# Gated graph network and graph attention, 64 graphs: layer 1's values by seven block products in place of eight, a later norm and half words for the younger pair, and shared small buffers

## The chip, the cores and the metric

The kernel runs on one core of one Trainium2 chip. The metric is the device time of one execution in microseconds (us). A NeuronCore has a matrix engine (TensorE, PE in the profile; its weight loads are listed apart as PEld), a vector engine (VectorE, DVE), a scalar engine (ScalarE, ACT), a third elementwise engine (GpSimd, POOL) and a queue that issues DMAs (SyncE, SP). Each takes its own instructions in program order and waits on semaphores for the others. Below, "the chip's time" is the median of three runs, and "span" is what the hardware profiler saw of one execution.

## What is computed

There are 64 graphs of 256 nodes with 256 features each, in float32, and an integer adjacency matrix for each. Two layers follow each other, both with a layer norm and a relu ahead and a residual behind. Layer 0 is a gated graph network of three steps (messages, an aggregation over the edges, a GRU cell); layer 1 is graph attention with four heads of 64 features.

```python
h = jnp.maximum(_layernorm(x), 0.0)
x = x + L0(h, adj, ...)             # 3 x: m = h @ weight[i]; aggr = A^T m; h = gru(aggr, h)
h = jnp.maximum(_layernorm(x), 0.0)
h = (h @ W.T + b).reshape(B, 256, 4, 64)                    # layer 1's values
logits = leaky_relu(l_src[:, :, None] + l_dst[:, None], 0.2)   # l_src, l_dst: h with a_src, a_dst
probs = softmax(where(adj == 1, logits, -9e15), axis=2)
x = x + einsum('bijh,bjhc->bihc', probs, h)
```

The change concerns the line of layer 1's values. The kernel computes it with the scores in one product: the weights `w_val` have VW = 268 columns, four times 64 value columns and a column that gives the softmax denominator, and eight more for `l_src` and `l_dst`.

## The kernel before

Graphs go in pairs (PB = 2 graphs, 512 nodes, KN = 2 blocks of 128 nodes in each graph, KD = 2 blocks of 128 features); there are 32 pairs. Nothing is scheduled by a tool: each piece of work is a Python function that is put down with a tick, a phase and a pair (`at`, L340), and at the end all pieces are emitted tick by tick; within a tick first STEP, then READY, then REST, and within a phase the younger pair first. The order in which an engine meets its instructions is thus written out by hand. Pairs follow each other by 18 ticks (`APART`). A pair needs three steps of six ticks in layer 0 (`Step.tick_0` to `tick_5`, at its ticks 0 to 5, 12 to 17 and 24 to 29), and the next pair's steps fill the gaps, so every tick holds one STEP.

A tick's STEP is mostly PE: blocks of four float32 products of 128x128 by 128x256 (`block`, L327) and single ones (`part`, L463). `tick_2` (L516) ends with a chain over three engines: PE writes `qb` from `hT`, DVE adds bias and a kept term to it into `hn` (L524), ACT then writes another quarter of `hn` from the same bank (`state_n`, L466). READY and REST carry the work of other pairs beside it: `back` (L882) turns a state back into rows on PE (`pback`, L900), after which ACT casts it (`hNhi`, L890) and DVE takes the rest (`hNlo`, L891).

The values of pair p (all but the last three pairs, 29 of 32: `dma_b`) are at its ticks 43 and 44, in REST, where pair p+1 is in `tick_1` and `tick_2` of its last step, and pair p+2 in its `back`:

```python
for r in (r0, r0 + 1):                                  # values, L950
    pt = bank(f"pv_{p}_{r}")
    for k in range(KD):
        nc.tensor.matmul(pt[:, :VW], hb["hT"][:, k, ts(r, P)], w_val[:, k, :], ...)   # L960
    nc.vector.scalar_tensor_tensor(v["val"][:, r, :], pt[:, :VW], rstd, b_val, ...)    # L965
nc.vector.tensor_copy(v["score"][:, r0 : r0 + 2, :], v["val"][:, r0 : r0 + 2, S0:])    # L973
```

The relu'd rows come from DMA transposes: `plan_norm` gives `xn`, `plan_turn` splits it into half words (`words`, L401), writes them to DRAM, reads them back transposed into the buffer `turned` (SP, L407) and joins them (`hT`, L413). At tick 45 `score_rows` follows: PE transposes the scores (`pscore`, L983), DVE copies them to `flat` (L985), and SP writes them to DRAM and reads them back on all partitions (`drow`, L1003). They feed the maxima (`any`, L1045) from tick 49 on.

At the same ticks 43 to 46 of pair p stands the layer 0 norm of pair p+3, three pairs younger: at its own tick -10 the normed rows (L367), at -9.5 their relu on ACT (L859), at -9 the half words (L401), at -8 the transposing read and at -3 the join.

Small buffers: `any` (the maxima's unused full output) and `flat` have one buffer each; `o` (a quotient that DVE writes, L611, and POOL adds to x, L616) has two; the tags of the `small` pool have four.

Of the kernel before, what the change touches and what calls it, by code (L numbers as in the profile page):

```python
# [9 lines left out]
F32 = mybir.dt.float32  # L10
# [8 lines left out]
P = 128  # L19
# [8 lines left out]
def gated_gnn_then_gat_kernel(  # L28
# [47 lines left out]
    PB = 2  # L76
# [2 lines left out]
    VC = C + 1  # L79
    S0 = H * VC  # L80
    VW = S0 + 2 * H
    NPAIR = B // PB

    assert PB == 2 and KD * N == 512
# [178 lines left out]
    a_exp = const.tile([P, KD, 2 * H], F32, name="a_exp")  # L263

    bcol = const.tile([P, KD], F32, name="bcol")
    nc.gpsimd.memset(a_exp, 0.0)
    nc.gpsimd.memset(b_val, 1.0)

# [22 lines left out]
    def value_weights():  # L291
        pts = [bank(f"pwv_{k}") for k in range(KD)]
        pa = bank("pwa")
        for k in range(KD):
            for g in range(KD):
                nc.tensor.transpose(pts[k][:, ts(g, P)], w_nat[:, g, ts(k, P)], ident)
        for k in range(KD):
            for g in range(KD):
                nc.tensor.matmul(
                    pa[:, ts(k, 2 * H)], w_nat[:, g, ts(k, P)], a_exp[:, g, :],  # L300
                    start=(k == 0 and g == 0), stop=(g == KD - 1), skip_group_check=True,
                )
        for k in range(KD):
            nc.tensor.matmul(
                pa[:, ts(KD, 2 * H)], bmat[0][:, k, :], a_exp[:, k, :],
                start=False, stop=(k == KD - 1), skip_group_check=True,
            )
        for k in range(KD):
            nc.vector.tensor_copy(
                w_val[:, k, :S0].rearrange("q (h c) -> q h c", h=H)[:, :, :C],  # L310
                pts[k][:, :D].rearrange("q (h c) -> q h c", h=H),
            )
            nc.vector.tensor_copy(w_val[:, k, S0:], pa[:, ts(k, 2 * H)])
        nc.vector.tensor_copy(b_val[:, S0:], pa[:, ts(KD, 2 * H)])


    def flat(y):
# [26 lines left out]
    def plan_norm(src, name, p, ticks, relu=False):  # L344


        v = {}

        def stats(r0):
            def fn():  # L350
                if not v:
                    v["st"] = small.tile([P, R, 6], F32, tag="st", name=f"st_{name}")
                    v["mv"] = small.tile([P, R, 2], F32, tag="mv", name=f"mv_{name}")
# [247 lines left out]
    def divided(p, r, v, add, scalar=False):  # L601

        heads = v["po", r][:, :S0].rearrange("q (h c) -> q h c", h=H)
        rden = small.tile([P, H], F32, tag="rden", name=f"rden_{p}_{r}")
# [16 lines left out]
    def plan_tail(t0, p, v, g, turn_back, residual):  # L621
# [13 lines left out]
                nc.scalar.activation(v["link"][:, i, :, :], pt, AF.Identity, scale=1 / 16)  # L635

        def stats(i):
            st = small.tile([P, KN, 6], F32, tag="st", name=f"st_b{p}_{i}")
            mv[i] = small.tile([P, KN, 2], F32, tag="mv", name=f"mv_b{p}_{i}")
# [102 lines left out]
        def maxima(i):  # L742
            for h_ in range(H):
                for r in range(i * KN, (i + 1) * KN):
                    any_ = buf("any", [P, N], f"any_{p}_{r}_{h_}")
                    nc.vector.tensor_tensor_reduce(
                        any_, two(drow[i][h_ // 2])[:, h_ % 2, :], v["noedge"][:, r, :], 1.0, -3.0e38,
                        ALU.add, ALU.max, accum_out=v["top"][:, r, h_ : h_ + 1],
                    )
            t = v["top"][:, xs[i], :]  # L750
            nc.vector.tensor_add(t, t, v["val"][:, xs[i], S0 : S0 + H])
            nc.vector.scalar_tensor_tensor(t, t, ALPHA, t, op0=ALU.mult, op1=ALU.max)
            nc.vector.tensor_scalar(t, t, barred, -1.0, op0=ALU.max, op1=ALU.mult)
# [14 lines left out]
        def last_rows():  # L768

            r, i, s, n = R - 1, PB - 1, KN - 1, H // 2  # L770
            for y in range(2):
# [8 lines left out]
                rden = small.tile([P, n], F32, tag="rden", name=f"rden_{p}_{r}_{y}")  # L780
# [47 lines left out]
    def plan_pair(p):  # L828
# [5 lines left out]
        def ready(t, fn):  # L834
            at(t0 + t, READY, p, fn)
# [16 lines left out]


        dma_a = p >= 1
        norm_ticks = (-14, -13, -13, -9.6 if p == 1 else -10) if dma_a else (-14, -13, -13, -7)
        xn_a = plan_norm(lambda: v["x"], f"a{p}", p, [t0 + t for t in norm_ticks])
        ready(-1 if p else -2.8, to_edge)
        if dma_a:
            ready(-9.5, lambda: nc.scalar.activation(flat(xn_a["xn"]), flat(xn_a["xn"]), AF.Relu))  # L859

            h = plan_turn(
                lambda: xn_a["xn"], "hT_a", f"a{p}", p, [t0 - 8.9 if p == 1 else t0 - 9, t0 - 8, t0 - 2 if p == 3 else t0 - 3],
                joins=nc.scalar.copy if p == 3 else nc.vector.tensor_copy,
            )
        else:
            h = plan_relu_T(xn_a, "hT_a", f"a{p}", p, [t0 - 4, t0 - 3])
# [86 lines left out]
        def values(r0):  # L953
            def fn():
                if r0 == 0:
                    v["val"] = buf("val", [P, R, VW], f"val_{p}")
                for r in (r0, r0 + 1):
                    pt = bank(f"pv_{p}_{r}")
                    for k in range(KD):
                        nc.tensor.matmul(  # L960
                            pt[:, :VW], hb["hT"][:, k, ts(r, P)], w_val[:, k, :],
                            start=(k == 0), stop=(k == KD - 1),
                        )
                    if dma_b:
                        nc.vector.scalar_tensor_tensor(  # L965
                            v["val"][:, r, :], pt[:, :VW], xn_b["rstd"][:, r : r + 1], b_val,
                            op0=ALU.mult, op1=ALU.add,
                        )
                    else:
                        nc.vector.tensor_add(v["val"][:, r, :], pt[:, :VW], b_val)  # L970
                if r0 == 0:
                    v["score"] = small.tile([P, R, 2 * H], F32, tag="score", name=f"score_{p}", bufs=2)
                nc.vector.tensor_copy(v["score"][:, r0 : r0 + 2, :], v["val"][:, r0 : r0 + 2, S0:])  # L973
            return fn

        rest(37 + later, values(0))
        rest(38 + later, values(2))

        def as_rows(src, n, what):

            m = R * n
            pt = bank(f"p{what}_{p}")
            nc.tensor.transpose(pt[:m, :P], flat(src), ident)  # L983
            fl = buf("flat", [m, P], f"{what}_{p}")
            nc.vector.tensor_copy(fl, pt[:m, :P])  # L985
            rows = dram.tile([PB, n, N], F32, tag=what, name=f"{what}_dram_{p}")
            for r in range(R):
# [51 lines left out]
        def maxima(r, h0):  # L1039
            def fn():  # L1040
                if r == 0 and h0 == 0:
                    v["top"] = small.tile([P, R, H], F32, tag="top", name=f"top_{p}", bufs=2)
                for h in (h0, h0 + 1):
                    any_ = buf("any", [P, N], f"any_{p}_{r}_{h}")
# [131 lines left out]
```

## Time and profile before

| | before |
|---|---|
| chip's time, median of 3 (lowest to highest) | 2470.12 us (2470.04 to 2470.18) |
| profiled execution, its own time | 2470.13 us |
| its span | 2468.3 us |
| PEld busy | 2181.3 us (88%) |
| DVE busy | 1982.7 us (80%) |
| ACT busy | 1443.9 us (58%) |
| POOL busy | 494.9 us (20%) |
| DMA | 314.77 MB, mean 128 GB/s |
| values' products, L960, pv<-w_val,hT_b | 496 records, 122.4 us |
| values' bias and scale on DVE, L965 | 116, 51.7 us |

A float32 product shows as two records on PE, since the weights are loaded twice, so the 496 records of L960 are 248 products: eight in each of 31 pairs, the last pair's being at another line. Of the execution's 2470.13 us the span covers 2468.3, and 1.8 us lie around it. [...] the distance between starts is what a product costs.

### The profile page before, as it was taken

The page shows a single profiled execution, that of the slowest core. Times are in us where ns is not written, and L with a number is a line of the kernel's source. Part 1 is how long each engine was busy: PE and PEld are TensorE (multiplying, and loading weights), DVE is VectorE, ACT ScalarE, POOL GpSimd, SP SyncE. Part 2 cuts the span into 40 slices and gives each one's busy share as a digit, 9 for nine tenths or more (in the row PEclk, how much of TensorE's full clock was granted, in tenths as well). Part 3 has the DMA queues.
Part 4 walks back from the last instruction along what each step waited for, and adds up shares of the span by engine and source line. Part 5 has one row for each costly group of instructions (what it writes and reads, how often), then busy time and mean ns, then how long its engine had stood idle before and what let it go on. Part 6 is the DMA issues. An engine that isn't in the chain of part 4 may idle for free.

```text
span 2468.3 us, 37534 instructions
## 1 busy us (share of the span) xinstructions
PE 2452.6 (99%) x13417; PEld 2181.3 (88%) x13418; DVE 1982.7 (80%) x4662; ACT 1443.9 (58%) x3025; POOL 494.9 (20%) x422
## 2 busy tenths in 40 slices
PE   9999999999999999999999999999999999999999
PEld 7888888888898888888888988888888889888888
DVE  6778887788877888877888777888778887788777
ACT  4456555655556655556555566555565555665566
POOL 0011212122121212121221212121211212121122
PEclk9999999999999999999999999999999999999999
DMA  3135565645655655656456566557564565655456
GB/s 97 43 81 130 128 155 115 154 120 124 143 132 134 143 115 129 155 118 153 117 126 144 127 139 140 117 129 150 122 153 118 125 146 123 143 134 123 98 119 135
DMA packets 324859, 314.77 MB, mean 128 GB/s; under 512 B 168688, under 2 KB 284992, under 8 KB 324672
## 3 DMA queue, kind: packets, MB, share of 16 engines
q0 software_dynamic: 33728, 130.03, 28.0%
q1 hardware_dynamic: 288576, 181.55, 27.7%
q8 instruction: 106, 1.74, 0.3%
q10 hardware_dynamic: 2368, 0.79, 0.2%
q14 instruction: 81, 0.66, 0.1%
HBM read 215.62 MB, written 57.12 MB: 110 GB/s over the span
## 4 chain that ended last, share of the span: by engine, by line
PE 83%; DVE 12%; ACT 3%; issue 1%; DMA 1%; POOL 0%; SPq 0%; ACTq 0%; DVEq 0%; POOLq 0%
PE pd L327 18%; PE pn L327 13%; PE pc L327 9%; PE po L596 9%; PE pe L327 7%; PE pa L492 5%; PE qb L463 5%; PE p L327 5%; PE pv L960 5%; PE qa L463 4%; PE pback L900 2%; DVE hT_a L582 2%; DVE R L581 2%; DVE any L1045 2%; DVE hNlo L891 1%; ACT zz L1065 1%
## 5 line engine op out<-in xcount | busy, mean ns | idle before, releaser
L327 PE MATMUL pn<-aggr,w_a 128*128 128x256 f32 x1536 | 364.9, 380 | 0.2 <-DVE pn L548 0.2
L327 PE MATMUL pd<-T,w_a 128*128 128x256 f32 x1536 | 364.5, 380 | 0.0
L563 POOL TENSOR_TENSOR R<-hT_a,hn 128x512 f32<-128x512 f32 x95 | 139.9, 1473 | 1090.5 <-ACT hn L559 1053.1
L327 PEld LDWEIGHTS pn<-aggr,w_a 128*128 128x128 f32 x1536 | 286.8, 190 | 41.3 <-issue 0.7
L327 PEld LDWEIGHTS pd<-T,w_a 128*128 128x128 f32 x1536 | 287.0, 190 | 37.0
L596 PEld LDWEIGHTS po<-val,zz 128*128 128x128 f32 x2032 | 243.2, 192 | 5.6 <-ACT zz L1080 1.1
L581 DVE SCALAR_TENSOR_TENSOR R<-Z,R 128x512 f32<-128x512 f32 x192 | 132.5, 690 | 141.8 <-POOL R L563 127.6
L616 POOL TENSOR_TENSOR x<-x,o 128x256 f32<-128x256 f32 x126 | 137.9, 1096 | 534.4 <-DVE o L611 532.1
L559 ACT ACTIVATE hn<-pn,bi 128x256 f32<-128x256 f32 x384 | 160.4, 470 | 142.9 <-PE pn L327 142.8
L596 PE MATMUL po<-val,zz 128*128 128x65 f32 x2032 | 240.5, 272 | 0.7 <-ACT zz L1080 0.7
L1065 ACT ACTIVATE zz<-zz,val 128x256 f32<-128x256 f32 x496 | 223.9, 505 | 0.5 <-DMA zz<-score_dram 0.5
L1045 DVE CUSTOM_DVE_ANT_0 any<-drow,noedge 128x256 f32<-128x256 f32 x496 | 208.2, 420 | 11.1 <-DMA drow<-score_dram 2.4
L470 ACT ACTIVATE R<-pc,brz 128x256 f32<-128x256 f32 x192 | 80.5, 470 | 220.5 <-PE pc L327 220.5
L548 DVE SCALAR_TENSOR_TENSOR pn<-R,hn 128x512 f32<-128x512 f32 x192 | 148.1, 771 | 74.7 <-ACT R L470 53.1
L470 ACT ACTIVATE R<-pe,brz 128x256 f32<-128x256 f32 x192 | 80.4, 470 | 214.0 <-PE pe L327 214.0
L327 PE MATMUL pd<-T,w_h 128*128 128x256 f32 x768 | 184.4, 383 | 3.5 <-DVE pe L532 0.5
L327 PE MATMUL p<-T,w_a 128*128 128x256 f32 x768 | 181.6, 379 | 0.0
L327 PE MATMUL pe<-aggr,w_a 128*128 128x256 f32 x768 | 181.4, 379 | 0.0
L327 PE MATMUL pc<-aggr,w_a 128*128 128x256 f32 x768 | 181.4, 379 | 0.0
L327 PE MATMUL pc<-hT_a,w_h 128*128 128x256 f32 x768 | 181.4, 379 | 0.0
L891 DVE TENSOR_TENSOR hNlo<-pback,hNhi 128x512 fp32r<-128x512 f32 x128 | 88.2, 690 | 114.1 <-ACT hNhi L890 114.1
L327 PEld LDWEIGHTS pd<-T,w_h 128*128 128x128 f32 x768 | 143.5, 190 | 33.3 <-DVE pe L532 15.0
(199 smaller groups left out, 5312.0 us busy)
## 6 DMA issues: line engine op xcount, KB each, us to landing
zz<-score_dram POOLq DMA_DIRECT2D x62, 1024.0 KB, 10.7
zz<-topT_dram POOLq DMA_DIRECT2D x62, 1024.0 KB, 8.0
adj<-in_adj_dram SPq DMA_DIRECT2D x64, 512.0 KB
drow<-score_dram SPq DMA_DIRECT2D x62, 512.0 KB
x<-in_x_dram SPq DMA_DIRECT2D x32, 512.0 KB
words_dram_a<-words_a SPq DMA_DIRECT2D x31, 512.0 KB
out_dram<-x SPq DMA_DIRECT2D x31, 512.0 KB
words_dram_b<-words_b SPq DMA_DIRECT2D x29, 512.0 KB
```

The costliest lines, as they stand in the source:

```text
L327: nc.tensor.matmul(pt[:, ts(c, N)], w[:, k, j * D + c * P : j * D + (c + 1) * P], src[:, k, :], start=start and c == 0 and k == 0, stop=(c ...
L463: nc.tensor.matmul(pt, w_n[:, j, :], src, start=start, stop=True, skip_group_check=True)
L470: nc.scalar.activation(of(dst, i)[:, c, :], src[:, c, :], AF.Tanh, bias=brz[:, g0 + c : g0 + c + 1], scale=0.5)
L492: nc.tensor.matmul(pt[:, ts(i, N)], hN[half][:, i * KN + s, ts(e, P)], edge[:, i * KN + s, :], start=(s == 0 and half == 0), stop=(s == KN ...
L548: nc.vector.scalar_tensor_tensor(by_c(self.bank(f"pn{i}")), of(self.R, i), 1.0, of(self.hn, i), op0=ALU.add, op1=ALU.mult)
L559: nc.scalar.activation(n__[:, c, :], p_n[:, c, :], AF.Tanh, bias=bi[:, 2 * KD + c : 2 * KD + c + 1])
L563: nc.gpsimd.tensor_sub(of(self.R, i), of(self.hT(), i), n__)
L581: nc.vector.scalar_tensor_tensor(d_, of(self.Z, i), 1.0, d_, op0=ALU.add, op1=ALU.mult)
L596: nc.tensor.matmul(po[:, ts(h_, VC)], zz[:, j, h_, ts(s, P)], v["val"][:, i * KN + j, ts(h_, VC)], start=(j == 0), stop=(j == KN - 1),)
L616: add(v["x"][:, r, :], v["x"][:, r, :], o)
L1045: nc.vector.tensor_tensor_reduce(any_, drow[r // KN][:, h, :], v["noedge"][:, r, :], 1.0, -3.0e38, ALU.add, ALU.max, accum_out=v["top"][:, ...
L1065: nc.scalar.activation(zz[:, h, :], zz[:, h, :], AF.Prelu, alpha=ALPHA, bias=v["val"][:, r, S0 + H + h : S0 + H + h + 1],)
```

## The change

Layer 1's values of the 29 pairs are computed by a scheme of seven products of half width. Let a graph's operand have the blocks x00, x01, x10, x11 (first index: half of the nodes, second: half of the features) and the weights w00, w01, w10, w11 (half of the features, half of the 268 columns, VH = 134). The eight block products of before (as four of 268 columns in a graph) become seven of 134 columns. Four sums of weight blocks are made once (`w_val_sum`), four sums of operand blocks in every pair (`value_sums`, for both graphs together), and the seven products land in three parts of one bank. Between them ACT copies parts from one place to another (L1007 to L1009, L1015) and DVE adds (L1016, L1024); in before the sums were made by PE's accumulation alone. The scale and bias (L1026) follow, in one operation for each of the four row blocks as before. The `score` copy is one for both graphs, at the end. The pieces stand at tick 43 (READY `value_sums`, REST `values_1` for both graphs) and 44 (READY `values_2`, REST `values_3`), and the sums use the `turned` buffer.

For pairs 3 and up the layer 0 norm's result moves from tick -10 to -8.4, its relu from -9.5 to -8.3, the half words from -9 to -7.6 and the transposing read from -8 to -6.8; the join stays. `any` and `flat` now share the two buffers of `o`; `rden`, `st`, `mv` have two buffers in place of four, `score` one in place of two.

```diff
+    VH = VW // 2
...
+        w00, w01, w10, w11 = (w_val[:, k, ts(c, VH)] for k in range(KD) for c in range(2))
+        t1, t2, t3, t4n = (w_val_sum[:, j, :] for j in range(4))
+        nc.vector.tensor_sub(t1, w01, w00)
+        nc.vector.tensor_sub(t2, w11, t1)
+        nc.vector.tensor_sub(t3, w11, w01)
+        nc.vector.tensor_sub(t4n, w10, t2)
...
-                    any_ = buf("any", [P, N], f"any_{p}_{r}_{h_}")
+                    any_ = buf("o", [P, N], f"any_{p}_{r}_{h_}")
...
+        lag = 1.6 if p >= 3 else 0
+        norm_ticks = (-14, -13, -13, -9.6 if p == 1 else -10 + lag) if dma_a else (-14, -13, -13, -7)
...
+            ready(-9.5 + 1.2 * (p >= 3), lambda: nc.scalar.activation(flat(xn_a["xn"]), flat(xn_a["xn"]), AF.Relu))
...
+                [t0 - 8.9 if p == 1 else t0 - 7.6 if lag else t0 - 9, t0 - 6.8 if lag else t0 - 8, ...],
...
+        def value_sums():
+            S = v["S"] = buf("turned", [P, 4, PB, P], f"S_{p}")
...
+            nc.vector.tensor_add(S[:, 0], x10, x11)
+            nc.vector.tensor_sub(S[:, 1], S[:, 0], x00)
+            nc.vector.tensor_sub(S[:, 2], x00, x10)
+            nc.vector.tensor_sub(S[:, 3], x01, S[:, 1])
+
+        def values_1(e):
...
+            value_product(e, 0, x[:, 0, :P], w_val[:, 0, :VH], start=True)
+            value_product(e, 2, x[:, 1, P:], w_val_sum[:, 3, :])
+            value_product(e, 1, v["S"][:, 0, e, :], w_val_sum[:, 0, :])
+            other = v["val"][:, e * KN + 1, :]
+            nc.scalar.copy(other[:, VH:], pv[e][:, ts(1, VH)])
+            nc.scalar.copy(pv[e][:, ts(1, VH)], pv[e][:, ts(0, VH)])
+            nc.scalar.copy(other[:, :VH], pv[e][:, ts(2, VH)])
+
+        def values_2(e):
+            x = hb["hT"][:, :, ts(e, N)]
+            value_product(e, 1, v["S"][:, 1, e, :], w_val_sum[:, 1, :])
+            value_product(e, 0, x[:, 1, :P], w_val[:, 1, :VH])
+            nc.scalar.copy(pv[e][:, ts(2, VH)], pv[e][:, ts(1, VH)])
+            nc.vector.tensor_add(pv[e][:, ts(1, VH)], pv[e][:, ts(1, VH)], v["val"][:, e * KN + 1, VH:])
+
+        def values_3(e):
+            value_product(e, 2, v["S"][:, 2, e, :], w_val_sum[:, 2, :])
+            value_product(e, 1, v["S"][:, 3, e, :], w_val[:, 1, VH:])
...
+            nc.vector.tensor_add(halves, halves, pv[e][:, None, 2 * VH : 3 * VH].to_broadcast([P, 2, VH]))
+            for y, src, m in ((other, other, 1), (one, pv[e][:, :VW], 0)):
+                nc.vector.scalar_tensor_tensor(
+                    y, src, xn_b["rstd"][:, r + m : r + m + 1], b_val, op0=ALU.mult, op1=ALU.add
+                )
+            if e == PB - 1:
+                v["score"] = small.tile([P, R, 2 * H], F32, tag="score", name=f"score_{p}", bufs=1)
+                nc.vector.tensor_copy(v["score"], v["val"][:, :, S0:])
+
+        if dma_b:
+            ready(43, value_sums)
+            for e in range(PB):
+                rest(43, lambda e=e: values_1(e))
+                ready(44, lambda e=e: values_2(e))
+                rest(44, lambda e=e: values_3(e))
...
-            fl = buf("flat", [m, P], f"{what}_{p}")
+            fl = buf("o", [P, N], f"{what}_{p}")[:m, :P]
```

More of the change, by code (lines that the diff above doesn't have):

```diff
@@ L265, in gated_gnn_then_gat_kernel @@
     bcol = const.tile([P, KD], F32, name="bcol")
+    w_val_sum = const.tile([P, 4, VH], F32, name="w_val_sum")
     nc.gpsimd.memset(a_exp, 0.0)
@@ L351, in fn @@
                 if not v:
-                    v["st"] = small.tile([P, R, 6], F32, tag="st", name=f"st_{name}")
-                    v["mv"] = small.tile([P, R, 2], F32, tag="mv", name=f"mv_{name}")
+                    v["st"] = small.tile([P, R, 6], F32, tag="st", name=f"st_{name}", bufs=2)
+                    v["mv"] = small.tile([P, R, 2], F32, tag="mv", name=f"mv_{name}", bufs=2)
                 for r in (r0, r0 + 1):
@@ L603, in divided @@
         heads = v["po", r][:, :S0].rearrange("q (h c) -> q h c", h=H)
-        rden = small.tile([P, H], F32, tag="rden", name=f"rden_{p}_{r}")
+        rden = small.tile([P, H], F32, tag="rden", name=f"rden_{p}_{r}", bufs=2)
         nc.vector.reciprocal(rden, heads[:, :, C])
@@ L637, in stats @@
         def stats(i):
-            st = small.tile([P, KN, 6], F32, tag="st", name=f"st_b{p}_{i}")
-            mv[i] = small.tile([P, KN, 2], F32, tag="mv", name=f"mv_b{p}_{i}")
+            st = small.tile([P, KN, 6], F32, tag="st", name=f"st_b{p}_{i}", bufs=2)
+            mv[i] = small.tile([P, KN, 2], F32, tag="mv", name=f"mv_b{p}_{i}", bufs=2)
             for s in range(KN):
@@ L779, in last_rows @@
                 heads = po[:, : n * VC].rearrange("q (h c) -> q h c", h=n)
-                rden = small.tile([P, n], F32, tag="rden", name=f"rden_{p}_{r}_{y}")
+                rden = small.tile([P, n], F32, tag="rden", name=f"rden_{p}_{r}_{y}", bufs=2)
                 nc.vector.reciprocal(rden, heads[:, :, C])
@@ L854, in plan_pair @@
         dma_a = p >= 1
-        norm_ticks = (-14, -13, -13, -9.6 if p == 1 else -10) if dma_a else (-14, -13, -13, -7)
+        lag = 1.6 if p >= 3 else 0
+        norm_ticks = (-14, -13, -13, -9.6 if p == 1 else -10 + lag) if dma_a else (-14, -13, -13, -7)
         xn_a = plan_norm(lambda: v["x"], f"a{p}", p, [t0 + t for t in norm_ticks])
@@ L858, in plan_pair @@
         if dma_a:
-            ready(-9.5, lambda: nc.scalar.activation(flat(xn_a["xn"]), flat(xn_a["xn"]), AF.Relu))
+            ready(-9.5 + 1.2 * (p >= 3), lambda: nc.scalar.activation(flat(xn_a["xn"]), flat(xn_a["xn"]), AF.Relu))
             h = plan_turn(
-                lambda: xn_a["xn"], "hT_a", f"a{p}", p, [t0 - 8.9 if p == 1 else t0 - 9, t0 - 8, t0 - 2 if p == 3 else t0 - 3],
+                lambda: xn_a["xn"], "hT_a", f"a{p}", p, [t0 - 8.9 if p == 1 else t0 - 7.6 if lag else t0 - 9, t0 - 6.8 if lag else t0 - 8, t0 - 2 if p == 3 else t0 - 3],
                 joins=nc.scalar.copy if p == 3 else nc.vector.tensor_copy,
@@ L963, in fn @@
                         )
[L964 to L970, printed above, removed]
+                    nc.vector.tensor_add(v["val"][:, r, :], pt[:, :VW], b_val)
                 if r0 == 0:
-                    v["score"] = small.tile([P, R, 2 * H], F32, tag="score", name=f"score_{p}", bufs=2)
+                    v["score"] = small.tile([P, R, 2 * H], F32, tag="score", name=f"score_{p}", bufs=1)
@@ L973, in fn @@
                 nc.vector.tensor_copy(v["score"][:, r0 : r0 + 2, :], v["val"][:, r0 : r0 + 2, S0:])
             return fn
-        rest(37 + later, values(0))
-        rest(38 + later, values(2))
+        pv = {}
+        def value_sums():
+            S = v["S"] = buf("turned", [P, 4, PB, P], f"S_{p}")
+            x00, x01, x10, x11 = (
+                hb["hT"].rearrange("q k (e m n) -> q k m e n", e=PB, m=KN)[:, k, m] for m in range(2) for k in range(KD)
+            )
[3 more added lines that the diff above has]
+            nc.vector.tensor_sub(S[:, 3], x01, S[:, 1])
@@ new lines, in value_product @@
+        def value_product(e, part, x, w, start=False):
+            nc.tensor.matmul(pv[e][:, ts(part, VH)], x, w, start=start, stop=True, skip_group_check=True)
+        def values_1(e):
+            if e == 0:
+                v["val"] = buf("val", [P, R, VW], f"val_{p}")
+            pv[e] = bank(f"pv_{p}_{e}")
+            x = hb["hT"][:, :, ts(e, N)]
[6 more added lines that the diff above has]
+            nc.scalar.copy(other[:, :VH], pv[e][:, ts(2, VH)])
@@ new lines, in values_2 @@
+        def values_2(e):
+            x = hb["hT"][:, :, ts(e, N)]
+            value_product(e, 1, v["S"][:, 1, e, :], w_val_sum[:, 1, :])
[5 more added lines that the diff above has]
+            value_product(e, 1, v["S"][:, 3, e, :], w_val[:, 1, VH:])
+            r = e * KN
+            one, other = (v["val"][:, r + m, :] for m in range(KN))
+            halves = other.rearrange("q (c w) -> q c w", c=2)
+            nc.vector.tensor_add(halves, halves, pv[e][:, None, 2 * VH : 3 * VH].to_broadcast([P, 2, VH]))
+            for y, src, m in ((other, other, 1), (one, pv[e][:, :VW], 0)):
+                nc.vector.scalar_tensor_tensor(
+                    y, src, xn_b["rstd"][:, r + m : r + m + 1], b_val, op0=ALU.mult, op1=ALU.add
+                )
+            if e == PB - 1:
+                v["score"] = small.tile([P, R, 2 * H], F32, tag="score", name=f"score_{p}", bufs=1)
+                nc.vector.tensor_copy(v["score"], v["val"][:, :, S0:])
@@ L979, in as_rows @@
+        if dma_b:
[4 more added lines that the diff above has]
+                rest(44, lambda e=e: values_3(e))
+        else:
+            rest(37, values(0))
+            rest(38, values(2))
         def as_rows(src, n, what):
@@ L1043, in fn @@
                 for h in (h0, h0 + 1):
-                    any_ = buf("any", [P, N], f"any_{p}_{r}_{h}")
+                    any_ = buf("o", [P, N], f"any_{p}_{r}_{h}")
                     nc.vector.tensor_tensor_reduce(
```

## The prediction, on record before the result

> **What bounds the kernel now.** I read the page's busy times, then the chain of waits, then PE's groups with shapes apart, then the timeline at the ticks of the change.
>
> ```profile
> PE 2452.6 (99%) x13417; PEld 2181.3 (88%) x13418; DVE 1982.7 (80%) x4662; ACT 1443.9 (58%) x3025; POOL 494.9 (20%) x422
> ...
> PE 83%; DVE 12%; ACT 3%; issue 1%; DMA 1%; POOL 0%; SPq 0%; ACTq 0%; DVEq 0%; POOLq 0%
> ```
>
> PE is bound throughout. The distances between its record starts add up to the span but for about 20 us, so a product removed is gained, and a wait that PE doesn't have today is lost whole: no later slack takes it back. What PE has at the values (groups with shapes apart):
>
> ```profile
> L596 PE MATMUL po<-val,zz 128*128 128x65 f32 x2032 | 240.5, 272 | 0.7 <-ACT zz L1080 0.7
> L960 PE MATMUL pv<-w_val,hT_b 128*128 128x268 f32 x496 | 122.4, 390 | 0.4 <-ACT hT_b L387 0.4
> L900 PE MATMUL pback<-ident,hT_a 128*128 128x128 f32 x768 | 115.2, 273 | 0.3 <-DVE hT_a L582 0.2
> ```
>
> Each row idles under 1 us in 31 pairs. The timeline of one pair, from the last single product of `tick_2` to the scores (start, length):
>
> ```profile
> 1219.97 0.59 PE L463 MATMUL qb<-hT_a,w_n 128*128 128x256 f32 x2
> ...
> 1220.40 0.60 PE L900 MATMUL pback<-ident,hT_a 128*128 128x128 f32 x4
> 1220.61 0.48 DVE L524 SCALAR_TENSOR_TENSOR hn<-qb,bhn,m5n 128x256 f32<-128x256 f32 x1 [0.19 <-PE qb L463]
> ...
> 1220.84 1.97 PE L960 MATMUL pv<-w_val,hT_b 128*128 128x268 f32 x8
> ...
> 1221.12 0.47 ACT L466 ACTIVATE hn<-qb,bhn 128x256 f32<-128x256 f32 x1 [0.80 <-DVE hn L524]
> 1221.49 1.05 ACT L1018 ACTIVATE zz<-link 128x1024 f32<-128x1024 bf16 x1
> ...
> 1222.44 0.57 ACT L890 CAST hNhi<-pback 128x512 fp32r<-128x512 f32 x1
> ...
> 1223.05 0.69 DVE L891 TENSOR_TENSOR hNlo<-pback,hNhi 128x512 fp32r<-128x512 f32 x1 [0.34 <-ACT hNhi L890]
> 1223.66 0.89 DVE L965 SCALAR_TENSOR_TENSOR val<-pv,rstd_b,b_val 128x268 f32<-128x268 f32 x2
> ...
> 1224.58 0.17 DVE L973 COPY score<-val 128x16 f32<-128x16 f32 x1
> 1224.67 0.69 DVE L532 TENSOR_TENSOR pe<-pd,m 128x512 f32<-128x512 f32 x1
> ...
> 1226.10 0.27 PE L983 MATMUL pscore<-ident,score 128*32 128x128 f32 x1
> ```
>
> The reader is to see two things. PE has no gap here. And the scores are ready at 1224.58 + 0.17 = 1224.75, while PE comes for them at 1226.10: a reserve of 1.35 us, on DVE, behind a chain PE, DVE `hn`, ACT `hn`, ACT `link`, ACT `hNhi`, DVE `hNlo`. The trace's records have the same distances in all 29 pairs, to 0.01 us, every 75.5 us. So one pair, worked out, times 29 is the result.
>
> [...] the two `pv` groups of eight and what lies between start at 226 ns a record[...], 216 for 256 columns, 109 for `pback` (128 columns). [...] the trace's copies of 256 and 512 columns take 377 and 589 ns, 0.83 an element.
>
> **The products.** Before: 8 products, 16 records at 226 ns, 3.62 us a pair. After: 14 products of 134 columns, 28 records. No row has this width. Lower bound 114 ns[...]. Upper bound 120 ns, which the aggregation's records (L492) show[...]. I take 114: 28 x 0.114 = 3.19, gain 0.43 us a pair, 12.5 us in 29. At 120 it is 0.26 and 7.5.
>
> **What DVE and ACT get.** Estimates by the rows: an ACT copy of 134 columns 0.277 us (0.377 less 122 x 0.83 ns; 0.2 to 0.377 as bounds); DVE in PSUM on 134 columns 0.305 (256: 0.43), on 268 columns 0.427, scaled and biased 0.487 from PSUM and 0.44 from SBUF, the sums of 256 columns 0.42, `score` 0.19. A pair gets 8 ACT copies, 2.2 us, and on DVE 4 sums, 2 + 2 additions, 4 scalings and a copy, 5.2 us where 4 scalings and two small copies took 2.3. Neither engine is full; place decides.
>
> **Tick 43 is covered.** `value_sums` (1.5 us pipelined) begins after DVE's T2 (ends 1215.43) and ends by 1216.9; PE needs the first sum at 1216.46, and DVE's next, `hNlo`, waited till 1218.11 anyway. ACT's six copies stand behind `hNhi` (ends 1218.08) and end by 1219.7; `tick_2`'s block and two single products keep PE busy till 1219.96 with the next `values_2` behind. Its products find their copies done. Cost nothing; without the block's cover PE, done with `values_1` at 1217.37, would wait 2.3 us. It is done 0.44 us earlier than before (12 records of 114 ns in place of 8 of 226).
>
> **Tick 44 is not.** Zero is PE's start of the group `qb<-hT_a` (before 1219.97). Before: `pscore` at 6.13, T4n 6.24, the RZ block (`pd<-T,w_h`) at 6.67.
> - First wait. PE does `values_2` to 1.34 and `pback` to 1.78. DVE `hn` ends at 1.12, ACT `hn` at 1.62; only then, ACT being in order, the copy L1015 (to 1.80), then DVE's addition L1016 (to 2.14), which `values_3` needs. PE waits 0.4 us, to 2.20. Behind it stand the S2 and RA blocks. They end, and PE is at `pscore`, at 2.20 + 0.91 + 3.45 = 6.56, with 0.1 for the reload of weights after a wait 6.66. Before's one such wait (T4n to `pd<-T,w_h` at 1201.36, for `pe`) shows the 0.1: its second record follows by 0.32 in place of 0.22.
> - Second wait. The two copies push ACT's `link` and `hNhi` by 2 x 0.18; `hNlo` runs 3.44 to 4.13. Behind it on DVE: addition 4.05 to 4.48, scaling to 4.95, scaling to 5.35, addition to 5.70, scaling to 6.17, scaling to 6.57, `score` 6.60 to 6.79. With before's two scalings and a copy it ended at 4.78. PE's `pscore` starts at 6.85 and, with the reload, T4n at about 7.06, RZ at 7.49. DVE's `pe` ends at 7.39, just in time.
> So PE is 7.49 - 6.67 = 0.82 later on this leg and 0.44 earlier on the first: +0.38 us a pair, x 29 = 11.0 us. (At 120 ns: +0.44.)
>
> **Behind it.** DVE then has `pe`, three state sums, the flat copy, the moved `xn` (1.37 us), `pn0`: ends about 10.76, wanted by PE at 7.49 + 3.45 = 10.94. It fits by 0.2. The relu of `xn` now stands on ACT ahead of the tanh from `pe` (R), which delays `pn1` to about 13.1, wanted at 14.4. It fits; cost nothing, and if these covers fail, 0.2 to 1 us a pair.
>
> **The moved steps' DMAs.** On SP the words' write (0.5 MB) and its transposing read now come after the four score writes and two `drow` reads. The words are made some 6 us later; before, the read was issued at 1231.78, its transfers landed a median 7.6 us later (longest 11.4), and the join stood at 1248.58. A reserve of 5 us, 1.7 at worst. `drow` and the score writes no longer stand behind the words[...]. On POOL nothing is passed. Nothing taken.
>
> **Small buffers.** `any` now waits for POOL's addition two `o` before: POOL started it at 1248.01, 0.1 after the quotient, and the next `any` is at 1251.46. `flat`'s DMAs are four ticks ahead of the next `o`. Taken at nothing, up to 0.3 us a pair of DVE time that PE doesn't see. The four weight sums once: about 1 us of DVE. Neither end of the run is in the 29 pairs: 0 to 1 us.
>
> **Rivals.**
> - Only the first wait shows (copies at 0.2, DVE's six shorter by the bounds' sum): 6.66 - 6.13 - 0.44 = +0.09 us, 2.6 in all: no change, 2473. For it: all DVE durations are estimates. Against: 0.2 us is far below any row of that width. 12%.
> - Faster: the two sets of copies meet no wait, and the products' gain stays: 2470.1 - 12.5 = 2457.6. Place: `values_3`. It decides if L1015 and L1016 are done by 1.78 rather than 2.14, and `score` by 6.1 rather than 6.79. For it: DVE and ACT are 80% and 58% busy, so there is room in sum. Against: ACT's `hn` ends at 1.62 whatever the copies cost, and both follow. 8%.
> - Larger: the fit of 0.2 at `pn0` fails, or the join's transfer is late beside the score traffic, or `any` waits for DMA; 1 us a pair, 29 us: 2499. Against: the reserves above. 10%.
>
> **How the numbers follow.** The sum is made against the profiled 2470.13 (span 2468.3 and 1.8 around it), the same as the median 2470.12. Forecast: 2470.1 + 11.0 = 2481, 70%. Its own range by the bounds (copies +-0.1, DVE +-0.15, reload 0 to 0.1, spacing to +0.07 a pair) is +0.13 to +0.65 us, 2474 to 2489. The whole range 2473 to 2490 leaves out the faster case and the larger one. Within 0.2% (about what measurement can tell) is 2465.2 to 2475.1: chance 0.12. Faster 0.08, slower 0.80.
>
> **What would show it.** Records of 134 columns 114 to 120 ns apart; PE waits at `values_3` of 0.4 us for DVE L1016, and at `pscore` of 0.2 to 0.3 for `score`, in all 29 pairs; none at `values_1`, `values_2` and `pn`; DVE busy near 2067 us, ACT near 1510. It is wrong if PE meets `values_3` or `pscore` without a wait, or if the period of a pair isn't 75.9 us.

## The result, and the profile after

| | before | after |
|---|---|---|
| chip's time, median (lowest to highest) | 2470.15 us (2470.04 to 2471.47), 4 runs | 2593.76 us (2572.02 to 2624.35), 4 runs |
| ratio to before, 95% interval | | 1.047 (1.039 to 1.055) |
| profiled execution, its span | 2468.3 us | 2622.5 us |
| granted TensorE clock, mean | 1.0 | 0.983 |

The changed kernel is slower by 124 us, where 11 were forecast. The ratio leaves out the profiled execution, which at 2624.35 us is over 1.5% above the fastest and counts as slow; the median of the other three is 2584.02 us, 114 above before. The four executions differ by 2%, and the profiled one is the longest, so a time of it is compared below with the medians only where its spread doesn't matter.

The page after, with busy times and the chain of waits:

```profile
PE 2483.5 (95%) x13766; PEld 2195.8 (84%) x13766; DVE 2042.4 (78%) x4869; ACT 1498.5 (57%) x3257; POOL 496.8 (19%) x422
...
PEclk9999999999899999999999999999999899999999
...
PE 69%; DVE 13%; DMA 12%; ACT 5%; issue 1%; POOL 0%; SPq 0%; DVEq 0%; ACTq 0%; POOLq 0%
PE pd L335 13%; PE pn L335 13%; DMA turned_a<-words_dram_a 12%; PE pc L335 9%; PE pa L500 6%; PE po L604 6%; PE p L335 5%; PE qb L471 5%; PE qa L471 4%; PE pe L335 3%; PE pback L910 2%; DVE val L1026 2%; DVE xn_a L375 2%; PE pv L996 2%; DVE pn L556 1%
```

PE is at 95% in place of 99, two slices have a clock below full, and a DMA has come into the chain: the transposing read of the younger pair's half words, 12% where DMA had 1. The waits (total us, times, longest) name what PE stands for:

```profile
PEld pn L335 <- DVE pn L556: 121.8, 46, 12.8
PE pn L335 <- DVE pn L556: 106.4, 45, 12.7
DVE hT_a L421 <- DMA turned_a<-words_dram_a: 102.7, 16, 15.5
...
ACT xn_a L869 <- DVE xn_a L375: 48.5, 30, 1.8
...
PEld pscore L1047 <- PE pc L335: 18.2, 29, 0.8
```

Of PE's 45 waits for `pn` some 30 last about 1.2 us and come once in a pair; seven last 4.6 to 12.7 us. They have different causes. The distance from one pair's `pscore` to the next (the period, below) tells them apart: before, it was 75.49 us in all pairs but those at the two ends of the run; after, it is 77.30 in the quiet pairs, and 79 to 93 in about half of all pairs.

**A quiet pair.** The timeline after, from the RZ block on (start, length, engine, line):

```profile
906.60 1.97 PE L335 MATMUL pd<-T,w_h 128*128 128x256 f32 x8
...
907.90 1.36 DVE L375 TENSOR_SCALAR xn_a<-x,mv_a,rstd_a 128x256 f32<-128x256 f32 x4
...
908.40 1.89 PE L335 MATMUL pe<-aggr,w_a 128*128 128x256 f32 x8
909.29 1.06 ACT L869 ACTIVATE xn_a<-xn_a 128x1024 f32<-128x1024 f32 x1 [1.65 <-DVE xn_a L375]
...
910.25 0.46 ACT L474 ACTIVATE hn<-qb,bhn 128x256 f32<-128x256 f32 x1
...
910.75 0.70 DVE L556 SCALAR_TENSOR_TENSOR pn<-R,hn 128x512 f32<-128x512 f32 x1 [1.49 <-ACT hn L474]
...
911.50 1.99 PE L335 MATMUL pn<-aggr,w_a 128*128 128x256 f32 x8 [1.21 <-DVE pn L556]
```

ACT idles 1.65 us until DVE has the normed rows, then does their relu (L869). Only behind it comes `hn` (L474), an operand of the older pair's `pn` on DVE, and PE waits 1.21 us for that, in every quiet pair.

**A late join.** Windows of the profile after, round the longest wait of DVE (columns: window, its length, busy time and count of PE, PEld, DVE, ACT and POOL, the granted clock, the share of the DMA engines, GB/s):

```profile
670.00:683.00 13.00, 13.00 (x81) 11.87 (x80) 10.49 (x27) 7.92 (x14) 1.92 (x2) 1.00 1.15 108
683.00:698.00 15.00, 8.20 (x54) 7.52 (x52) 0.00 (x0) 3.93 (x7) 0.00 (x0) 0.91 1.11 76
698.00:712.00 14.00, 8.09 (x28) 6.77 (x28) 13.46 (x32) 2.71 (x7) 5.24 (x4) 0.61 0.15 46
712.00:740.00 28.00, 28.00 (x157) 24.99 (x156) 24.63 (x61) 17.80 (x43) 5.15 (x4) 1.00 0.51 127
```

From 683 to 698 DVE does nothing: its next instruction is the join. PE runs out of work at 691. When the join is done at 699.6 and PE resumes at 703.91, the granted clock is at half (0.50 in the windows from 699.60 to 703.91 and from there to 707.70), and the first `pn` block takes 3.78 us where 1.89 are usual. The time is lost a second time. The trace's half-clock spells last 3.4, 6.8, 10.2 or 13.7 us, and eight of the ten ahead of the run's end begin within waits of PE of 4.6 to 12.7 us. The other two begin behind shorter waits, of 2.40 and 1.06 us, while in experiment 6 the 29 waits of 1.2 us leave the clock at 1.000; what decides for a short wait is not shown. PE is busy for 40.7 us in the ten spells, so about 20 us of this execution, by an estimate of half of that, are the slower clock.

The transposing read, in the view of its tile: minimum, median and maximum ns of its issue on SP, and who waited. First before, then after:

```profile
L407 SPq DMA_TRANSPOSE turned_a<-words_dram_a x31: 1851/4928/6025, 57.9 to 2287.7; - x31
...
DMA turned_a<-words_dram_a: 0.4, 1
```

```profile
L415 SPq DMA_TRANSPOSE turned_a<-words_dram_a x31: 1430/6325/12855, 58.1 to 2445.6; - x31
...
DMA turned_a<-words_dram_a: 110.4, 17
```

Its last transfer landed a median 7.6 us after the issue before (longest 11.4), and 13.6 after (longest 29.3). In before, the read is issued at 1231.78 and the first of POOL's two additions of 1 MB into `zz` (the score adds) 3.1 us later, at 1234.90; over the pairs the median is 4.2 us later. In after, it is 916.20 for the read and 915.67 for the addition, and over the pairs the addition is a median 0.8 us ahead. The read now mostly comes into a transfer that has begun.

### The profile page after: what moved, and what is told of

Read it like the earlier page. It is cut to its first block, busy times and chain, and to the rows that moved or that the text cites. A ratio compares the mean times of both kernels' runs of the same rounds, so it can differ in the third digit from the quotient of the medians.

```text
span 2622.5 us, 38682 instructions
## 1 busy us (share of the span) xinstructions
PE 2483.5 (95%) x13766; PEld 2195.8 (84%) x13766; DVE 2042.4 (78%) x4869; ACT 1498.5 (57%) x3257; POOL 496.8 (19%) x422
## 4 chain that ended last, share of the span: by engine, by line
PE 69%; DVE 13%; DMA 12%; ACT 5%; issue 1%; POOL 0%; SPq 0%; DVEq 0%; ACTq 0%; POOLq 0%
PE pd L335 13%; PE pn L335 13%; DMA turned_a<-words_dram_a 12%; PE pc L335 9%; PE pa L500 6%; PE po L604 6%; PE p L335 5%; PE qb L471 5%; PE qa L471 4%; PE pe L335 3%; PE pback L910 2%; DVE val L1026 2%; DVE xn_a L375 2%; PE pv L996 2%; DVE pn L556 1%
## 5 line engine op out<-in xcount | busy, mean ns | idle before, releaser
L335 PE MATMUL pn<-aggr,w_a 128*128 128x256 f32 x1536 | 382.9, 394 | 106.4 <-DVE pn L556 106.4
L335 PEld LDWEIGHTS pn<-aggr,w_a 128*128 128x128 f32 x1536 | 292.1, 196 | 164.7 <-DVE pn L556 121.8
L1109 DVE CUSTOM_DVE_ANT_0 any<-drow,noedge 128x256 f32<-128x256 f32 x496 | 188.4, 418 | 3.2 <-DMA drow<-score_dram 3.2
## 6 DMA issues: line engine op xcount, KB each, us to landing
zz<-score_dram POOLq DMA_DIRECT2D x62, 1024.0 KB, 11.7
```

Of the source, the lines that this page charges most:

```text
L335: nc.tensor.matmul(pt[:, ts(c, N)], w[:, k, j * D + c * P : j * D + (c + 1) * P], src[:, k, :], start=start and c == 0 and k == 0, stop=(c ...
L1109: nc.vector.tensor_tensor_reduce(any_, drow[r // KN][:, h, :], v["noedge"][:, r, :], 1.0, -3.0e38, ALU.add, ALU.max, accum_out=v["top"][:, ...
```

## The experiments

**1. The shared buffers alone** (the kernel before with `any` and `flat` in `o`, and the `small` tags at 2, 2, 2 and 1).

```diff
-                    any_ = buf("any", [P, N], f"any_{p}_{r}_{h}")
+                    any_ = buf("o", [P, N], f"any_{p}_{r}_{h}")
...
-            fl = buf("flat", [m, P], f"{what}_{p}")
+            fl = buf("o", [P, N], f"{what}_{p}")[:m, :P]
```

> The kernel before with the shared small buffers alone (any and flat in o, two buffers for rden, st, mv, one for score). Both theories: no effect, 2469 to 2472 us. A third (any and flat now wait for POOL or DMA and hold DVE): over 2475 us.

Measured: 2463.07 us (2462.82 to 2463.70), ratio 0.9971 (0.9959 to 0.9982). The expectation missed: sharing gains 7.4 us. The timelines show how. Before, two successive maxima, their accumulator reads between:

```profile
1198.58 0.42 DVE L1045 CUSTOM_DVE_ANT_0 any<-drow,noedge 128x256 f32<-128x256 f32 x1
1198.92 0.08 DVE L1045 DVE_READ_ACCUMULATOR2_ANT top<- 128x1 f32 x1
1199.04 0.42 DVE L1045 CUSTOM_DVE_ANT_0 any<-drow,noedge 128x256 f32<-128x256 f32 x1
```

With shared buffers:

```profile
1195.58 0.42 DVE L1045 CUSTOM_DVE_ANT_0 any<-drow,noedge 128x256 f32<-128x256 f32 x1
1195.92 0.08 DVE L1045 DVE_READ_ACCUMULATOR2_ANT top<- 128x1 f32 x1
1195.92 0.42 DVE L1045 CUSTOM_DVE_ANT_0 any<-drow,noedge 128x256 f32<-128x256 f32 x1
```

The starts are 0.46 us apart before and 0.34 now. With one buffer the second maximum waits on a semaphore of its own engine until the first is done (the trace's record carries that wait), since both write the same place; that nobody reads the place changes nothing. With two buffers this wait is gone. The gain reaches PE at one place: ahead of the block `pd<-T,w_h` PE stood 8.06 us in 28 pairs for DVE's `pe` in the kernel before, and stands 1.24 with shared buffers (in both cases the sum over how much later a record starts than the usual distance). The view of weight loads has the same place, before and with shared buffers:

```profile
PEld pd L327 <- DVE pe L532: 15.0, 29, 0.9
```

```profile
PEld pd L327 <- DVE pe L532: 8.0, 28, 0.7
```

**2. Which of the shared buffers** (the kernel before, `any` in `o`, nothing else).

```diff
-                    any_ = buf("any", [P, N], f"any_{p}_{r}_{h}")
+                    any_ = buf("o", [P, N], f"any_{p}_{r}_{h}")
```

> The kernel before, where only the unused output of the row maximum (any) takes the double buffer of o in place of its own single one; the flat tile and the small tiles stay as they were. Theory A (the 7.4 us gained by the shared buffers come from successive maxima that no longer wait for each other's write): 2462 to 2464.5. Rival B (they come from the small tiles or the flat tile): 2469 to 2471.

Measured: 2464.12 us (2463.68 to 2464.27). Theory A. The order of the instructions in the trace is the same as before on DVE, ACT, POOL and SP; the buffer of `any` alone carries about 6.2 of the 7.4 us. What the last 1 us comes from was not tested.

**3. The later norm taken back** (the changed kernel without the move of norm, relu, words and read).

```diff
-        lag = 1.6 if p >= 3 else 0
+        lag = 0
...
-            ready(-9.5 + 1.2 * (p >= 3), lambda: nc.scalar.activation(flat(xn_a["xn"]), flat(xn_a["xn"]), AF.Relu))
+            ready(-9.5, lambda: nc.scalar.activation(flat(xn_a["xn"]), flat(xn_a["xn"]), AF.Relu))
```

> The changed kernel with the younger pair's norm, relu, half words and transposing read back at their old ticks; seven products and shared buffers stay. Theory A (the late norm does the harm: the relu of xn stands on ACT ahead of hn, which pn0 waits for, and the transposing read is issued behind the score adds and lands late): no join waits for turned_a, no wait of PE for pn0 over 0.2 us; what is left are the waits at values_3, now 1.2 us since xn stands on DVE ahead of L1016, less the products' 0.44: about +0.9 us a pair, 2490 to 2502 us, and repeatable to 1 us. Theory B (DVE and ACT work of the seven products is the cause, whatever the order): 2550 us or more.

Measured: 2489.66 us (2489.40 to 2490.01), 0.3 us below theory A's range; B falls. The late joins and the waits at `pn` are gone, so the moved steps carry about 104 of the 124 us (by the medians of all executions). But the products now cost more than the forecast said for them, 26.6 us over the shared buffers alone. PE's waits and the timeline of this run:

```profile
PE pv L996 <- DVE pv L1016: 30.9, 29, 1.1
```

```profile
925.33 1.37 DVE L375 TENSOR_SCALAR xn_a<-x,mv_a,rstd_a 128x256 f32<-128x256 f32 x4
...
926.62 0.42 DVE L466 TENSOR_TENSOR T4n<-T2n,hT_a 128x256 f32<-128x256 f32 x1
...
926.95 0.51 DVE L1016 TENSOR_TENSOR pv<-pv,val 128x134 f32<-128x134 f32 x2
...
927.30 0.50 PE L996 MATMUL pv<-w_val_sum,S 128*128 128x134 f32 x2 [1.06 <-DVE pv L1016]
```

At its old place the norm's 1.37 us stand on DVE ahead of the addition that `values_3` waits for. The move takes 0.8 us of that wait from every pair (1.06 to 0.25), and costs far more behind.

**4. The later norm alone** (the kernel before with the moved norm, relu, words and read).

> The kernel before with the later norm, relu, half words and transposing read alone; values by eight products. Theory A: PE waits for pn0 by 1 to 1.5 us a pair, since relu then hn stand on ACT, and turned_a lands late in about half of the pairs, up to 15 us: 2540 to 2620 us, the runs tens of us apart. Theory B: 2470 to 2480 us.

Measured: 2579.55 us (2572.05 to 2585.63), ratio 1.044 (1.042 to 1.0461). The join waited for its read 17 times, 101.8 us in all: the loss needs no seven products. In the quiet pairs the period was 75.83, only 0.34 above before, where 1 to 1.5 were expected. DVE waits for `hn` here too (1.49 us), but the norm starts 0.63 us after `pscore` in place of 1.84, as DVE has less to do for the values and is ahead. So the relu ahead of `hn` costs PE its full 1.2 us only together with the products, and the expectation had taken the two for independent.

**5. Late words alone** (the kernel before, norm and relu at their old place, the words at -7 and the read at -6.8).

> The kernel before with only the half words (to tick -7) and the transposing read later, norm and relu where they were: it puts the words' write and the read where the changed kernel has them in time (7 us after the score product), with no other operation on ACT or DVE moved ahead of pn0. Theory A: no wait of PE for pn0; turned_a lands late in about half of the pairs and the join holds DVE, PE waits, 2500 to 2590 us, runs apart. If the score adds do not slow the transposing read: landing within 8 us of issue and 2470 to 2472 us.

Measured: 2503.94 us (2495.03 to 2509.82). The quiet pairs keep before's 75.49; about half of the pairs are late, up to 82.3. Here no engine's order of arithmetic changed but for DVE's words, and on SP their write and the read come later: the new place of these transfers costs 34 us by itself. Which transfer is in the way, experiment 6 shows.

**6. The score adds later** (the changed kernel; POOL's additions two ticks later, so behind the read).

```diff
-        rest(43 + later, add_rows(0, "score"))
-        rest(44 + later, add_rows(1, "score"))
+        rest(43 + later + 2 * dma_b, add_rows(0, "score"))
+        rest(44 + later + 2 * dma_b, add_rows(1, "score"))
```

> The changed kernel with one edit: POOL's two additions of 1 MB each into zz (the score adds) are issued two ticks later, so that the transposing read of the words is on its queues before them. Theory A (the large scattered part of the loss is the read landing behind those additions, the rest is the quiet pair's 77.3 us period): turned_a lands in time in all pairs, no period above about 77.5, so e3's 2463 plus 29 times 77.3 - 75.25 = 2.05, about 2522 us, repeatable to 2 us, granted clock back above 0.99. Rival B (the read is slow for another reason, its own queue or its place behind the words' write): still 2560 or more, scattered, with late joins.

Measured: 2523.02 us (2522.78 to 2523.16), within 1 us of theory A. The period is 77.30 in all pairs but one and those at the ends, the clock 1.000. The read's tile:

```profile
L415 SPq DMA_TRANSPOSE turned_a<-words_dram_a x31: 1308/1864/3282, 58.4 to 2345.4; - x31
...
DMA turned_a<-words_dram_a: 0.4, 1
```

Without the additions ahead of it the read lands a median 4.3 us after its issue (longest 5.4). What of the changed kernel's loss was random is this collision, 2593.8 - 2523.0 = 70.7 us in the median of four executions, 61.0 without the longest. What is left on PE, in the view of its waits:

```profile
PE pn L335 <- DVE pn L556: 35.0, 29, 1.2
PE pscore L1047 <- DVE score L1031: 7.2, 29, 0.4
PE pv L996 <- DVE pv L1016: 7.2, 29, 0.3
```

**7. The relu behind `hn` too** (the same, and the relu 0.6 tick later, the words after it).

```diff
-            ready(-9.5 + 1.2 * (p >= 3), lambda: nc.scalar.activation(flat(xn_a["xn"]), flat(xn_a["xn"]), AF.Relu))
+            ready(-9.5 + 1.8 * (p >= 3), lambda: nc.scalar.activation(flat(xn_a["xn"]), flat(xn_a["xn"]), AF.Relu))
```

> The run before with two more moves: ACT's relu of xn 0.6 tick later (behind hn of the older pair), and the two halves' words just after it. Theory A (in a quiet pair 1.2 to 1.4 us are lost because pn0's operand hn stands behind that relu on ACT): the wait of PE pn for DVE L556 goes, the period falls from 77.3 to 76.0 to 76.2, the total to 2487 to 2495. Rival B (pn0 is late because of R and T4n themselves, not of the relu): the period stays within 0.3 us of the previous run's, 2513 or more.

Measured: 2480.40 us (2479.83 to 2480.49), 42.6 less, and below the expected stretch: the period is 75.82. The waits of PE:

```profile
PE pscore L1047 <- DVE score L1031: 7.3, 29, 0.4
PE pv L996 <- DVE pv L1016: 7.2, 29, 0.2
```

The line of `pn` is gone. So one ACT operation of 1.06 us that stood ahead of another pair's `hn` cost 1.48 us a pair. What remains are the two waits of tick 44 that the prediction has.

**8. Are the two waits one?** (the same, and `hn` of the last layer's `tick_2` behind the copies L1015).

```diff
-            self.state_n(0, 1, q_b[:, N:])
+            if self.l < L - 1:
+                self.state_n(0, 1, q_b[:, N:])
...
+            if l == L - 1:
+                ready(t + 2.01, lambda g=g: g.state_n(0, 1, g.qb[:, N:]))
```

> The kernel of 2480.4 us (score adds later, relu later), with one edit: in the last layer the second state product (ACT hn of tick_2) is taken behind the copies of the first values, so that the addition that values_3 waits for can start sooner. Theory A (the two waits of tick 44 lie on one chain: what ends last is the score, behind hNhi and hNlo on ACT and DVE, which this edit doesn't move): the wait at values_3, 0.41 us a pair, goes, the wait at pscore grows by as much, and the total is 2477 to 2482. Rival B (the two waits add up and each can be had alone): 0.41 times 29 = 11.9 us less, 2468 to 2470. Rival C: hn taken later delays pe and what follows, 2485 or more.

Measured: 2477.37 us (2477.12 to 2477.73). PE's first wait went from 11.9 to 1.9 us (as sums of late starts, in 29 pairs), the second rose from 12.0 to 18.5:

```profile
PE pscore L1050 <- DVE score L1034: 13.7, 29, 0.6
```

Of 10.0 us that were freed, 6.5 came back some 5 us later on PE, at the next thing that DVE was late with. Mostly theory A; a third was had alone.

**9. The whole in another order** (the changed kernel with every part kept: `value_sums` at a fixed place in STEP, the norm behind it at -11 and the relu at -9.5, the words copied by ACT at -9.45, the read back at -8, `hn` behind the copies as in 8, and ACT's first `link` block of tick 44 later).

```diff
-            ready(43, value_sums)
+            step(43, value_sums)
...
-        norm_ticks = (-14, -13, -13, -9.6 if p == 1 else -10 + lag) if dma_a else (-14, -13, -13, -7)
+        norm_ticks = (-14, -13, -13, -9.6 if p == 1 else -11 if p >= 3 else -10) if dma_a else (-14, -13, -13, -7)
...
-                lambda: xn_a["xn"], "hT_a", f"a{p}", p, [t0 - 8.9 if p == 1 else t0 - 7.6 if lag else t0 - 9, t0 - 6.8 if lag else t0 - 8, ...],
+                lambda: xn_a["xn"], "hT_a", f"a{p}", p, [t0 - 8.9 if p == 1 else t0 - 9.45 if p >= 3 else t0 - 9, t0 - 8, ...],
+                halves=nc.scalar.copy if p >= 3 else nc.vector.tensor_copy,
...
-        ready(38 + later, barred_in(0, 0))
+        ready(38.7 + later if dma_b else 38, barred_in(0, 0))
```

> The changed kernel, all parts kept, in another order: the younger pair's xn at tick -11 behind value_sums, its relu at -9.5 and its words copied by ACT at -9.45, the turn back at -8, so ahead of the score adds; value_sums at a fixed place in the step; the last layer's second state product taken behind the copies of the first values; the first block at 38.7. Theory A (seven products save 12.5 us of PE, and all the loss is waits that the order makes): wait at values_3 gone, at pscore at most 0.2 us, none at pn, joins in time, period 74.9 to 75.1, so 2452 to 2460. Rival B (the additions of blocks on DVE and ACT cost the path time in any order): a wait of 0.4 us or more remains at pscore, 2463 to 2475. Rival C: the moved state product delays the score chain, above 2475.

Measured: 2457.18 us (2457.00 to 2457.62), ratio 0.9947 (0.9930 to 0.9964), period 75.00. This beats before and the shared buffers alone. The longest entry left in the view of weight loads is small, and no wait at the values, at `pscore` of these pairs or at `pn` is in it:

```profile
PEld pd L335 <- DVE pe L541: 8.4, 28, 0.6
```

**10. The same order with eight products** (9 with the values of the kernel before).

> The reordered kernel (2457.2), with eight products of blocks as in the kernel before in place of the seven, and without the sums and copies that go with them; every other part of the reordering stays. Theory A (the seven products are what the reordered kernel is faster by): PE's records take 13.0 us more and the small gaps behind the products, about 6 us, go, so 2462 to 2466, as with shared buffers alone. Rival B (the gain came from the other order): 2459 or less. Rival C (the other order costs something that the products pay for): 2468 or more.

Measured: 2464.01 us (2463.66 to 2464.54). Theory A. PE's records at their usual distances sum to 2441.9 us with eight products and 2429.1 with seven, 12.8 less; small gaps grow from 14.5 to 20.2 us, 5.0 of it among the values' own products and at their start. So seven products are worth 6.8 us in an order that covers them, and the other order by itself gains nothing (2464.0 beside 2463.1).

## Why the prediction was wrong

The ledger of the 123.6 us between the two medians, by steps from one kernel to the next (numbers of the experiments):

| term | from | us | forecast |
|---|---|---|---|
| shared buffers | before to 1 | -7.4 | 0 |
| seven products, waits of tick 44 | 1 to 7 | +17.3 | +11.0 |
| relu ahead of `hn` | 7 to 6 | +42.6 | 0 |
| read behind the score adds | 6 to after | +70.7 | 0 |

They sum to 123.2; the last row, and the sum with it, is 9.7 us smaller where the longest execution of the changed kernel is left out. The last two steps differ in one move each (7 also in the words, which follow the relu). Kernel 7 has the later norm and the later additions beside the products, so the 17.3 are theirs in that order.

That kernel 7's 2480.40 us lie beside the forecast 2481 is partly luck: the gain of the shared buffers, which the forecast had at nothing, offsets waits that it had 6.3 us too small.

- *The products.* Right. Their records start 114 ns apart; the values' own records take 12.1 us less and all of PE's 12.8, where 12.5 were forecast. As an estimate, before's trace gives the same 114: its records start 109 ns apart at 128 columns, 216 at 256 and 226 at 268, and a straight line through these is at 114 for 134. It does not hold for narrow ones: `po`, 65 columns, is at 112. A record itself lasts longer than this distance (390 ns at 268 columns), so it is the distances that are summed.
- *What DVE and ACT get.* Durations right to 0.03 us but for one: the copies took 0.272 and 0.255, DVE's additions 0.305 and 0.424, while the scaling with its source in SBUF took 0.498 where 0.44 was put. DVE was busy for 2042.4 us where 2067 were forecast; 19.8 of the difference are the maxima (208.2 us before, 188.4 after), which the shared buffers let overlap.
- *Tick 43 is covered.* Right: PE starts `values_2` with no wait.
- *Tick 44 is not.* Right in both places and in their order; the size was low. `values_3` started 2.19 us after the group `qb<-hT_a`, forecast 2.20. The score was done at 6.92, forecast 6.79, by the longer scalings, and PE took it 0.15 later, not 0.06: `pscore` at 7.07 and the RZ block at 7.61, forecast 6.85 and 7.49. The period rose by 0.57 (75.82 less 75.25) where 0.38 was reckoned; 0.12 of the difference are in these terms; where the other 0.07 are was not followed up.
- *Behind it.* Here the prediction failed first. It found that DVE reaches `pn0` 0.2 us before PE wants it, by DVE's own work, and said of the relu only that it delays R and `pn1`. `pn0` has a second operand, `hn` from ACT, and that was behind the relu, which itself waits for DVE's moved norm: a chain from DVE over ACT back to DVE. "0.2 to 1 us a pair" for a failing cover was too little as well; it was 1.48 (77.30 less 75.82).
- *The moved steps' DMAs.* The larger failure. "A reserve of 5 us, 1.7 at worst" took the landing times 7.6 and 11.4 from the old place of the read to a new one, where two additions of 1 MB begin beside it and it lands after 13.6 (median) to 29.3 us. The subtraction doesn't follow from the figures beside it (16.8 us from issue to join, less 6, less 7.6 or 11.4, is 3.2 or -0.6), but it comes near what the trace of after allows: the joins that were not held up start about 13 us after the read's issue. The queues that the step was moved past on SP were named, and POOL was dismissed with "nothing is passed": true of the words, not of the read, which had been issued a median 4.2 us ahead of the first addition and came 0.8 us behind it. That an addition takes more than 10 us to land was in the page of before (median 10.7).
- *Small buffers.* Wrong in sign. Only waits that sharing adds were looked for; the one that it removes, between two maxima, could be read in before's timeline, where the second maximum starts 0.12 us after the accumulator read of the first has started (1198.92 and 1199.04), and its record has a wait for DVE's own semaphore.
- *The rivals.* "Larger" named both true places, the fit at `pn0` and the join's transfer, and priced them at 1 us a pair, 29 us, with a chance of 10%. Together they were 113 us (42.6 and 70.7), 3.9 a pair.

Open: why the read is slow beside the additions. The runs show that it is (it lands a median 13.6 us after its issue beside them, and 4.3 in experiment 6, where they come later), and not by what.

## What to carry to other kernels

When a step moves, list for every consumer behind its new place all operands, on every engine, and not only the engine that moves; one elementwise operation ahead of another pair's operand cost 1.5 us a pair. A DMA's landing time belongs to its place (7.6 us at the old one here, 13.6 at the new): before it moves behind a large transfer of another queue, take the landing time from there, and count PE's slower restart on top (3.78 us in place of 1.89 for the block behind the longest wait). And a scratch output that nobody read still ordered its writers, at 0.12 us from one maximum to the next; give it two buffers (6.2 us in experiment 2).

## What had not been expected of the hardware

The read and the additions landed later beside each other (medians 13.6 us where 7.6 had been, and 11.7 where 10.7), and the DMA engines counted as full while less was moved. Windows of before, from the read's issue to the join, and of after, from the read's issue to the end of DVE's wait:

```profile
1231.80:1248.60 16.80, 16.80 (x98) 15.21 (x97) 11.63 (x30) 10.87 (x21) 4.20 (x4) 1.00 1.01 219
```

```profile
669.00:698.00 29.00, 22.20 (x137) 20.26 (x136) 11.46 (x28) 12.17 (x21) 2.49 (x3) 0.95 1.09 87
```

The DMA share is 1.01 and 1.09, both full, but 219 GB/s are moved in the one and 87 in the other. The longest landing of a score add rose from 15.9 to 28.4 us. It differs from pair to pair with the same program, which is where the spread of the changed kernel's runs comes from: 52 us between the shortest and the longest, and 0.4 in experiment 6, where the collision is gone.

A wait of a DVE instruction for its own engine's last one cost 0.12 us (0.46 against 0.34 between starts), here between two maxima with an accumulator read between them. Other operations were not tried.
